# A bidirectional Mamba-2 layer with a low-rank FFN: five short steps change their place in the order of four engines

## The chip, the cores and the metric

The kernel runs on one core of one Trainium2 chip. The metric is the device time of one execution in microseconds (us). Five engines work side by side and meet through semaphores: PE (TensorE, matrix products; PEld are its weight loads), DVE (VectorE), ACT (ScalarE), POOL (GpSimd) and SP (SyncE, which here only issues DMAs). Each of them runs its own instructions strictly in the order in which they were written.

## The reference, cut to what matters

The input x is 8 sequences of 512 tokens with 256 features, all in float32. For each of two directions d (the second reads the sequence backwards):

```python
h0 = layernorm(x)
z, xBC, dt = split(h0 @ Win)               # 512, 640 and 8 columns
xs, B, C = split(silu(conv4(xBC) + convb)) # causal, 4 taps, per channel
dt = softplus(dt + dtb); dA = exp(-exp(Alog) * dt)
h_t = dA_t * h_(t-1) + dt_t * B_t x_t      # 8 heads of 64, state 64
y = C_t h_t + D * xs
y = y * silu(z)
y = y * rsqrt(mean(y * y) + 1e-5) * normw
out_d = y @ Wout
```

Then `x = x + concat(out_0, out_1) @ Wo + bo`, and last `x = x + FFN(layernorm(x))`, where `FFN(u) = u @ W.T + b + (u @ V_r) @ C.T`.

## The kernel before, in words

Each sequence is cut into four chunks of 128 tokens. A `Pair` is one chunk of the forward direction with the mirrored chunk of the backward one, so there are 8 x 4 = 32 pairs, and the main loop (L817 to L936) has one iteration for each, i = 4b + c. An iteration finishes pair i (`p`), prepares pair i+1 (`q`), does a part of the projections and convolutions of a later sequence (`work`, up to four `Block`s of 128 channels from the table `todo`), and carries the tails of finished chunks: a `Tail` is 128 tokens of output, from the product with the output weights to the FFN and the store. `t` holds the tails that begin in this iteration, `t0` those that began in the one before. `before` is pair i-1.

The steps that matter here, with their engines:

- `outputs` (L557, PE, L563): y of a pair. For c > 0 first the part that comes from the state, which reads the state `h` and the decays already multiplied by C (`dec`), then the part within the chunk, which reads `lam` and `xdt`. Results go to two banks of PSUM (`py`).
- `evict` (L591, DVE, L593) adds y to D * xs; `times_gate` (L595, POOL, L597) multiplies by silu(z); `square` (L599, ACT) squares; `presum` (L616, POOL, L618 and L619), `norm_sum` (L602, PE, L605), `norm_mean` (L607, ACT, L609) and `norm_power` (L611, POOL, L612) make 1/rms.
- `decay_state` (L549, POOL, L553) and `add_state` (L577): the state of the next chunk. `add_state` is a product on PE (L583) and then an addition on DVE (L588), or for c = 0 a copy on ACT (L586).
- `turn` (L492): transposes of x on PE (L496) and a copy on ACT for each direction (L498). `scale_x` (L500, POOL, L507) multiplies these copies by dt; `scan` (L483, DVE, L490) and `mix` (L519, DVE, L520) make `lam`; `scale_c` (L476, POOL, L479) makes `dec`.
- `skip` (L524, ACT, L528): D * xs, four instructions for each direction. `gate` and `gate_silu` (L532 and L544): z on PE and its silu on ACT.
- Of a block: `project` (PE, L379), `tap` (ACT, L390: the first of the four taps), `convolve` (DVE, L397, three instructions), `silu` (ACT, L415, or L423 for B and C).
- Of a tail: `bias1` (POOL, L633) adds bo to x; `project` (PE, L640) and `residual` (DVE, L647, then the statistics of L221 and L222); `scales` (POOL, L229 to L232) and `norm2` (ACT, L657) the second layer norm; `bias2` (POOL, L668) adds b to x; `turn` (PE, L673, and ACT, L675), `ffn` (PE, L680), `add_ffn` (DVE, L683) and `store` (SP, L686).
- `prepare_wf` (L207): once, in i=2, the FFN's low-rank product is made on PE (L212) and added to W on DVE (L213).

What sets the order is the text itself: `pin` (L60) makes each instruction of an engine follow the one traced before it. PSUM is handed out in pools of a few banks: three for projections, gates and the state's product (`p_proj`), two for transposes and small products (`p_tr`), two for `py`, `pm`, `pf` and the prepared weights (`p_y`). A new use of a bank waits until the engine that empties it is done. The second p_y bank of an iteration is that of `pm`, which `residual` empties.

Of the kernel before, what the change touches and what calls it, by code (L numbers as in the profile page):

```python
# [10 lines left out]
ALU = mybir.AluOpType  # L11
# [3 lines left out]
P = 128  # L15
NB, L, DM = 8, 512, 256
NC = L // P
DI = 512
# [13 lines left out]
def tile_bimamba_ffn(  # L32
# [39 lines left out]
    pe, dve, act, pool, sp = nc.tensor, nc.vector, nc.scalar, nc.gpsimd, nc.sync  # L72
# [4 lines left out]
    p_proj = ctx.enter_context(tc.tile_pool(name="p_proj", bufs=3, space=PSUM))  # L77
# [10 lines left out]
    def ps(p, shape, name):  # L88
        return p.tile(shape, F32, name=name, tag=p.name)
# [4 lines left out]
    def load(b, chunks=1):  # L94
        xt[b] = xin.tile([P, NC, DM], F32, name=f"x_{b}", tag="x")
        for c in range(0, NC, NC // chunks):
            cs = slice(c, c + NC // chunks)
            sp.dma_start(out=xt[b][:, cs], in_=x[b].rearrange("(c p) d -> p c d", p=P)[:, cs])
# [96 lines left out]
    def prepare_wy(d, blks):  # L195

        wot, wo_sb = staged[d]
        for blk in blks:
            pw = ps(p_y, [P, DM], f"pwy_{d}_{blk}")
            for k in range(NK):  # L200
                pe.matmul(
                    pw, lhsT=wot[:, k, blk * P:(blk + 1) * P], rhs=wo_sb[:, k, :],
                    start=(k == 0), stop=(k == NK - 1),
                )
            dve.tensor_scalar(wy[:, d, blk, :], pw, normw_sb[:, d, blk:blk + 1], None, ALU.mult)

    def prepare_wf():  # L207

        wt_sb, vt_sb, ct_sb = staged["ffn"]
        for k in range(NK):  # L210
            pw = ps(p_y, [P, DM], f"pwf_{k}")
            pe.matmul(pw, lhsT=vt_sb[:, k * P:(k + 1) * P], rhs=ct_sb, start=True, stop=True)  # L212
            dve.tensor_tensor(wf[:, k, :], pw, wt_sb[:, k, :], ALU.add)  # L213
# [23 lines left out]
    def stats1(b, c0):  # L237

        seq[b]["mv"] = statistics(xt[b], NC, f"ln1_{b}", range(c0, c0 + 2), seq[b].get("mv"))

    def scales1(b):
        seq[b]["rsnm"] = scales(seq[b].pop("mv"), NC, f"ln1_{b}")

    def norm1(b):
        rs, nm = seq[b].pop("rsnm")
        for c in range(NC):
            act.activation(
                xt[b][:, c, :], xt[b][:, c, :], AF.Identity, bias=nm[:, c:c + 1], scale=rs[:, c:c + 1]
            )

    def turn1(b, k):

        if k == 0:
            seq[b]["xhT"] = seqp.tile([P, NK, L], F32, name=f"xhT_{b}", tag="xhT", bufs=3)
        pt = ps(p_tr, [P, L], f"pxh_{b}_{k}")
        for c in range(NC):
            pe.transpose(pt[:, c * P:(c + 1) * P], xt[b][:, c, k * P:(k + 1) * P], ident)
        act.copy(seq[b]["xhT"][:, k, :], pt)
        if k == NK - 1:
            xt.pop(b)  # L260
# [81 lines left out]
    def steps_last(b0):  # L342
        g = seq[b0]["g"]
        last = g["last"] = sm("last", b0, (P, 64))
        act.activation(last[F], fold[F], AF.Copy, scale=upto[F, P:])
        act.activation(last[W], fold[W], AF.Copy, scale=onward[W, 0:1])
# [92 lines left out]
    class Pair:  # L439
# [137 lines left out]
        def add_state(m):  # L577
            if m.c == NC - 1:
                return
            pst = ps(p_proj, [P, DI], f"pst_{m.name}")  # L580
            for d in range(2):
                rows = slice(d * NS, (d + 1) * NS)
                pe.matmul(pst[rows, :], lhsT=m.s["bn"][:, m.c, rows], rhs=m.xw[d], start=True, stop=True)  # L583
            if m.c == 0:
                m.h_new = m.tile("h", (P, DI))
                act.copy(m.h_new, pst)  # L586
            else:
                dve.tensor_tensor(m.h_new, m.h_new, pst, ALU.add)  # L588
            m.s["h"] = m.h_new

        def evict(m, d):  # L591
# [163 lines left out]
    q = pairs[0]  # L755
# [51 lines left out]
    def when(t, *what):  # L807
        for one in t if isinstance(t, list) else [t]:
            if one is not None:
                for w in what:  # L810
                    getattr(one, w)()

    def begun(at):
        return [tails[j] for j in range(n) if begin[j] == at]

    st = late = before = None
    for i in range(n):  # L817
        p, q = pairs[i], pairs.get(i + 1)
        b, c = order[i]
        t, t0 = begun(i), begun(i - 1)  # L820
        work = todo.get((b, c), [])
        work = work + [None] * (4 - len(work))
        even = b % NSG == 0

        ahead = b + 2 if even else b + 1
        if i + 2 < n:
            if not (st and not even and c == 2):
                pairs[i + 2] = Pair(*order[i + 2])
                pairs[i + 2].fetch()
        if (c == 0 if even else c == 1) and b + 3 < NB:  # L830
            load(b + 3)
        when(t0, "scales", "norm2", "bias2")
        p.decay_state()
        p.outputs()
        for d in range(2):
            p.evict(d)
            p.times_gate(d)
        p.add_state()
        when(before, "norm_sum", "norm_mean")
        if q:  # L840
            for d in range(2):
                q.turn(d)
        when(work[0], "project", "tap")
        when(t0, "turn")
        for d in range(2):
            p.square(d)
        if even and c in (1, 3) and ahead < NB:
            norm1(ahead + (c == 3))
        when(late, "silu")
        if st and not even and c == 2:  # L850
            st.exponential()
        if q:
            q.cb()
            q.gate(0)
            q.gate_silu(0)
            for d in range(2):
                q.scale_x(d)
            q.scan(0)
        if q:
            q.scan(1)  # L860
            q.skip(0)
        when(work[0], "convolve", "silu")
        if i < 2:
            prepare_wy(i, range(2))
        if q:
            q.mix(0)
            q.mix(1)
        if st and not even and c == 2:
            st.decays()
            steps_last(ahead)  # L870
            pairs[i + 2] = Pair(*order[i + 2])
            pairs[i + 2].fetch()
        when(t0, "ffn", "add_ffn")
        when(before, "norm_power")
        if q:
            q.scale_c()
        when(t, "bias1")
        p.presum()
        if st and not even and c == 2:
            st.weigh()  # L880
        when(t, "project", "residual")
        if even and 1 <= c <= 2 and ahead + 1 < NB:
            stats1(ahead + 1, 2 * c - 2)
        if even and c == 0 and ahead < NB:
            stats1(ahead, 2)
            if b == 0:
                stats1(ahead, 0)
            scales1(ahead)
        if not even and c == 3 and b + 3 < NB:
            stats1(b + 3, 0)  # L890
        if even and c == 2 and ahead + 1 < NB:
            scales1(ahead + 1)
        when(work[1], "project", "tap")
        if i < 2:
            prepare_wy(i, range(2, NBLK))
        if q:
            q.skip(1)
        when(work[1], "convolve")
        if i == 2:
            prepare_wf()  # L900
        if i == 0:
            steps_last(0)
            steps_total(0)
        if not even and c == 3 and ahead < NB:
            steps_total(ahead)
        if st and not even and c == 1:
            st.ratio()
            st.series()
        if q:
            q.gate(1)  # L910
            q.gate_silu(1)
        if even and c in (1, 3) and ahead < NB:
            turn1(ahead + (c == 3), 0)
            turn1(ahead + (c == 3), 1)
        if c == 2 and b + 1 < NB:
            tokenwise_b(b + 1)
        when(work[1], "silu")
        for w in work[2:]:
            when(w, "project", "tap", "convolve")
        if b == 0:  # L920
            when(work[3], "silu")
        if st and not even and c == 2:
            steps_by_token(ahead)
            st = None
        late, before = work[2], p
        if i + 2 < n:
            pairs[i + 2].fetch_dec()
        when(t0, "store")
        for j in range(n):
            if begin[j] == i + 1:  # L930
                tails[j] = Tail(*ends[j])
                tails[j].load()
        if even and c == 3 and ahead < NB:
            st = Steps(ahead, *steps_v(ahead))
        pairs.pop(i)
        pin()  # L936


    t, t0 = begun(n), begun(n - 1)
# [52 lines left out]
```

## Time and profile before

| what | value |
|---|---|
| time, median of 3 runs | 665.66 us (665.1 to 667.6) |
| the profiled execution's own time | 668.52 us |
| its span, first to last instruction | 666.5 us |
| PE busy | 623.3 us, 94% of the span |
| DVE busy | 542.0 us, 81% |
| POOL busy | 467.2 us, 70% |
| ACT busy | 399.8 us, 60% |
| mean granted clock of TensorE | 0.983 |

The profile is of one execution, so durations from it are set against 668.52 us. A busy share is a mean over the whole span; matmuls are pipelined, so a busy PE is not PE at its peak. Where an engine is idle, the profile names what ended the wait, inferred from semaphores; of several semaphores it names the one that came last by its records.

### The profile page before, as it was taken

How to read it: one execution, taken by the hardware profiler on the slowest of the kernel's cores; microseconds unless marked ns; L12 is line 12 of the kernel's file. 1: busy time of each engine (PE TensorE's matmuls, PEld its weight loads, DVE VectorE, ACT ScalarE, POOL GpSimd, SP SyncE). 2: the span in 40 equal slices, each digit the busy share in tenths (PEclk: the TensorE clock that was granted, in tenths of full speed). 3: DMA queues.
4: the chain of work that ended last, by engine and by line, in shares of the span. 5: the costliest groups of instructions: out<-in, count | busy, mean ns of one | idle time of the engine just before them, and what ended most of it. 6: DMA issues, size and time to landing. Idle time of an engine off the chain costs nothing.

```text
span 666.5 us, 12446 instructions
## 1 busy us (share of the span) xinstructions
PE 623.3 (94%) x4652; PEld 478.5 (72%) x4652; DVE 542.0 (81%) x827; ACT 399.8 (60%) x855; POOL 467.2 (70%) x572
## 2 busy tenths in 40 slices
PE   4968998999999999999999999999999998999996
PEld 2556676777776777877777677777877777787785
DVE  4788888788988899977988998877998887886643
ACT  2787565876566565875476574686576654564421
POOL 4447455677854888757856789638876679599983
PEclk9979998999999999999999998999999998999998
DMA  7555332313055312134045322332005432333010
GB/s 207 161 168 143 111 104 49 86 42 102 18 182 142 112 62 90 59 92 143 17 135 147 92 64 80 112 112 103 25 13 179 104 111 80 111 112 111 17 49 32
DMA packets 34940, 64.63 MB, mean 97 GB/s; under 512 B 7680, under 2 KB 22080, under 8 KB 34880
## 3 DMA queue, kind: packets, MB, share of 16 engines
q1 hardware_dynamic: 32736, 63.79, 31.8%
q8 instruction: 37, 0.61, 0.4%
q10 hardware_dynamic: 2144, 0.04, 0.2%
q14 instruction: 23, 0.19, 0.1%
HBM read 59.10 MB, written 4.72 MB: 96 GB/s over the span
## 4 chain that ended last, share of the span: by engine, by line
PE 51%; DVE 24%; POOL 13%; ACT 7%; issue 4%; DVEq 0%; POOLq 0%; ACTq 0%
PE pm L640 11%; PE pp L379 9%; PE pz L538 9%; PE py L563 9%; DVE xc L397 7%; DVE lam L490 4%; PE pf L680 3%; POOL yg L597 3%; DVE lam L520 3%; PE pxs L496 3%; POOL xdt L507 2%; PE pdt L275 2%; DVE x L647 2%; ACT xc L390 2%; PE pst L583 2%
## 5 line engine op out<-in xcount | busy, mean ns | idle before, releaser
L397 DVE SCALAR_TENSOR_TENSOR xc<-pp,conv_sb,xc 128x511 f32<-128x511 f32 x183 | 136.0, 744 | 46.3 <-ACT xc L390 41.9
L379 PE MATMUL pp<-xhT,win_sb 128*128 128x512 f32 x320 | 151.2, 600 | 0.5 <-ACT xhT L710 0.5
L490 DVE TENSOR_TENSOR_SCAN lam<-lam,seed 128x512 f32<-128x512 f32 x128 | 145.6, 1200 | 0.0
L538 PEld LDWEIGHTS pz<-xhT,win_sb 128*128 128x128 f32 x1024 | 125.7, 194 | 10.3 <-issue 7.7
L538 PE MATMUL pz<-xhT,win_sb 128*128 128x128 f32 x1024 | 126.6, 277 | 0.0
L640 PE MATMUL pm<-wy,yg 128*128 128x256 f32 x512 | 115.5, 379 | 0.0
L640 PEld LDWEIGHTS pm<-wy,yg 128*128 128x128 f32 x512 | 97.1, 190 | 13.1
L379 PEld LDWEIGHTS pp<-xhT,win_sb 128*128 128x128 f32 x320 | 57.8, 194 | 45.7 <-issue 42.6
L528 ACT ACTIVATE yg<-xc,dcol 128x128 f32<-128x128 f32 x256 | 80.9, 393 | 0.0
L390 ACT ACTIVATE xc<-pp,conv_sb 128x512 f32<-128x512 f32 x64 | 49.3, 774 | 44.9 <-PE pp L379 44.7
L520 DVE TENSOR_TENSOR lam<-lam,cb 128x1024 f32<-128x1024 f32 x64 | 75.0, 1212 | 0.1
L668 POOL TENSOR_TENSOR x<-x,bf_sb 128x256 f32<-128x256 f32 x32 | 23.3, 729 | 73.6 <-ACT xh L657 71.5
L507 POOL TENSOR_TENSOR xdt<-xs,dw 128x512 f32<-128x512 f32 x64 | 66.5, 1046 | 6.6 <-ACT xs L498 6.6
L563 PE MATMUL py<-lam,xdt 128*64 128x128 f32 x1024 | 66.3, 285 | 0.0
L415 ACT ACTIVATE xc<-xc 128x512 f32<-128x512 f32 x64 | 39.5, 628 | 43.7 <-DVE xc L397 43.4
L563 PEld LDWEIGHTS py<-lam,xdt 128*64 128x64 f32 x1024 | 58.6, 143 | 7.5 <-issue 4.6
L593 DVE TENSOR_TENSOR yg<-py,yg 128x512 f32<-128x512 f32 x64 | 42.2, 685 | 18.0 <-PE py L563 15.5
L507 POOL TENSOR_TENSOR xs<-xs,dw 128x512 f32<-128x512 f32 x48 | 50.1, 1045 | 3.8
L647 DVE SCALAR_TENSOR_TENSOR x<-pm,rms,x 128x256 f32<-128x256 f32 x64 | 30.9, 483 | 25.4 <-POOL x L633 16.5
L496 PE MATMUL pxs<-ident,xc 128*128 128x128 f32 x256 | 39.7, 286 | 12.5 <-ACT rms L609 5.1
L498 ACT COPY xs<-pxs 128x512 f32<-128x512 f32 x64 | 36.1, 586 | 15.4 <-PE pxs L496 15.2
L496 PEld LDWEIGHTS pxs<-ident,xc 128*128 128x128 f32 x256 | 29.8, 151 | 19.2 <-ACT rms L609 6.8
(445 smaller groups left out, 996.0 us busy)
## 6 DMA issues: line engine op xcount, KB each, us to landing
lam<-dat SPq DMA_DIRECT2D x64, 512.0 KB, 5.2
x<-in_x_dram SPq DMA_DIRECT2D x36, 128.0 KB, 2.2
out_dram<-x SPq DMA_DIRECT2D x32, 128.0 KB, 1.7
x<-in_x_dram SPq DMA_DIRECT2D x7, 512.0 KB, 6.8
win_sb<-in_win_dram SPq DMA_DIRECT2D x2, 640.0 KB, 5.8
win_sb<-in_win_dram SPq DMA_DIRECT2D x2, 512.0 KB, 7.9
wot<-in_wout_t_dram SPq DMA_DIRECT2D x2, 512.0 KB, 12.4
wo_sb<-in_wo_dram SPq DMA_DIRECT2D x2, 256.0 KB, 8.9
```

The source lines that it names most:

```text
L379: pe.matmul(pp, lhsT=win_sb[:, d, k, c0:c0 + P], rhs=s["xhT"][:, k, :], start=(k == 0), stop=(k == NK - 1),)
L390: act.activation(self.acc, self.pp, AF.Identity, bias=self.w[:, 4:5], scale=self.w[:, 3:4])
L397: dve.scalar_tensor_tensor(self.acc[:, to], self.pp[:, of], self.w[:, 3 - j:4 - j], self.acc[:, to], ALU.mult, ALU.add,)
L490: dve.tensor_tensor_scan(lam, lam, sd, 0.0, ALU.mult, ALU.add)
L496: pe.transpose(pt[:, blk * P:(blk + 1) * P], m.s["xc", d][:, blk, m.tcol[d]], ident)
L507: pool.tensor_tensor(hb(to), hb(m.xw[d]), dw[:, j, cols].unsqueeze(2).to_broadcast([P, NH, HD]), ALU.mult)
L520: dve.tensor_tensor(m.lam[d], m.lam[d], m.pcb[:, d, :].unsqueeze(1).to_broadcast([P, NH, P]), ALU.mult)
L528: act.activation(yg[:, blk, :], m.s["xc", d][:, blk, m.tcol[d]], AF.Copy, scale=dcol[:, d, blk:blk + 1])
L538: pe.matmul(pz[:, blk, :], lhsT=win_sb[:, d, k, blk * P:(blk + 1) * P], rhs=m.s["xhT"][:, k, m.tcol[d]], start=(k == 0), stop=(k == NK - 1),)
L563: pe.matmul(m.py[d][two * HD:(two + 1) * HD, blk, :], lhsT=lhsT, rhs=rhs, start=first, stop=last, skip_group_check=True,)
L640: pe.matmul(t.pm[:, d, :], lhsT=yg[:, blk, :], rhs=wy[:, d, blk, :], start=(blk == 0), stop=(blk == NBLK - 1),)
L647: dve.scalar_tensor_tensor(t.x1[:, 0, :], t.pm[:, d, :], t.s["rs", d, t.c], t.x1[:, 0, :], ALU.mult, ALU.add)
```

## The change

Five edits, all in the order of steps; no instruction is added or dropped.

1. `add_state` keeps its product on PE; its addition (or copy) becomes a step of its own, `new_state`, written after `norm_sum` and `norm_mean` of the pair before.
2. For every iteration that has a block to project, `norm2` is written behind the two `turn`s of `q` instead of at the head of the iteration, and `bias2` behind the `scale_x` of both directions. The four `scales` stay at the head. From i=27 on, where there is no block left, both stay where they were.
3. `bias1` is written ahead of `norm_power` and `scale_c` instead of behind them.
4. `prepare_wf` is written right after the projection of the second block of i=2 instead of after that block's convolution.
5. `skip(1)` of `q` is written behind `gate_silu(1)` and the `turn1` of a coming sequence instead of ahead of the second block's convolution.

```diff
         def add_state(m):
             if m.c == NC - 1:
                 return
-            pst = ps(p_proj, [P, DI], f"pst_{m.name}")
+            pst = m.pst = ps(p_proj, [P, DI], f"pst_{m.name}")
...
+
+        def new_state(m):
+            if m.c == NC - 1:
+                return
             if m.c == 0:
                 m.h_new = m.tile("h", (P, DI))
-                act.copy(m.h_new, pst)
+                act.copy(m.h_new, m.pst)
             else:
-                dve.tensor_tensor(m.h_new, m.h_new, pst, ALU.add)
+                dve.tensor_tensor(m.h_new, m.h_new, m.pst, ALU.add)
             m.s["h"] = m.h_new
...
-        when(t0, "scales", "norm2", "bias2")
+        when(t0, "scales")
+        if work[0] is None:
+            when(t0, "norm2", "bias2")
         p.decay_state()
...
         p.add_state()
         when(before, "norm_sum", "norm_mean")
+        p.new_state()
         if q:
             for d in range(2):
                 q.turn(d)
+        if work[0] is not None:
+            when(t0, "norm2")
         when(work[0], "project", "tap")
...
             for d in range(2):
                 q.scale_x(d)
+        if work[0] is not None:
+            when(t0, "bias2")
+        if q:
             q.scan(0)
...
         when(t0, "ffn", "add_ffn")
+        when(t, "bias1")
         when(before, "norm_power")
         if q:
             q.scale_c()
-        when(t, "bias1")
         p.presum()
...
         if i < 2:
             prepare_wy(i, range(2, NBLK))
-        if q:
-            q.skip(1)
+        elif i == 2:
+            prepare_wf()
         when(work[1], "convolve")
-        if i == 2:
-            prepare_wf()
...
             turn1(ahead + (c == 3), 0)
             turn1(ahead + (c == 3), 1)
+        if q:
+            q.skip(1)
         if c == 2 and b + 1 < NB:
             tokenwise_b(b + 1)
```

## The prediction, made before the changed kernel was seen

> **What bounds the kernel now.** I number the iterations of the main loop i = 0 to 31 (i = 4b + c). First I read busy time by stretch of the span: start and length, then the busy time of PE, PEld, DVE, ACT and POOL.
>
> ```profile
> 263.00:326.00 63.00, 63.00 (x524) 49.58 (x524) 53.36 (x80) 42.86 (x92) 44.12 (x56) 1.00 0.33 99
> 326.00:402.00 76.00, 71.52 (x529) 54.29 (x527) 67.93 (x107) 49.56 (x107) 55.69 (x65) 1.00 0.33 99
> 573.00:641.00 68.00, 64.48 (x600) 53.84 (x599) 47.12 (x63) 34.17 (x82) 57.50 (x69) 1.00 0.29 86
> ```
>
> The loop repeats every eight iterations (154.3 us between the gate products of i=8 and i=16, 215.37 and 369.69). In its first half (263 to 326, i=11 to 13) PE is never idle. In the second (326 to 402, i=14 to 17) PE stands idle 4.5 us and DVE is the fullest. In the last six iterations POOL is. Then I read PE's idle gaps, in the timeline of PE (start, duration, instruction, idle time before it and what ended it):
>
> ```profile
> 110.95 1.97 PE L563 MATMUL py<-dec__866,h__873 64*64 64x128 f32 x32 [2.41 <-POOL ln_nm L232]
> ...
> 367.85 0.66 PE L496 MATMUL pxs<-ident,xc 128*128 128x128 f32 x4 [1.09 <-ACT rms L609]
> ...
> 399.73 0.63 PE L257 MATMUL pxh<-ident,x 128*128 128x128 f32 x4 [1.11 <-DVE lam L520]
> ...
> 401.10 1.43 PE L563 MATMUL py<-dec__3705,h__3724 64*64 64x128 f32 x28 [0.38 <-DVE x L647]
> ```
>
> The first is at the start of i=3. POOL's ln_nm only happens to end nearby; DVE shows the cause:
>
> ```profile
> 108.24 2.29 DVE L397 SCALAR_TENSOR_TENSOR xc<-pp,conv_sb,xc 128x511 f32<-128x511 f32 x3
> 110.44 0.75 DVE L213 TENSOR_TENSOR wf<-pwf,wt_sb 128x256 f32<-128x256 f32 x2
> ```
>
> The outputs of i=3 need the two banks of p_y that hold the FFN weights' product; DVE empties them only after a convolution. The last gap (401.10) is the same bank rule: the residual (L647) empties the second one. What makes that residual late is in the chain of waits:
>
> ```profile
> 376.40 0.72 POOL rms L612
> 377.12 2.34 POOL dec__3525 L479
> 379.46 0.70 POOL x L633
> 380.16 0.02 issue
> 380.18 0.49 DVE x L647
> ```
>
> DVE waits for bias1 (L633), which is queued on POOL behind norm_power (L612) and scale_c (L479). The list of waits totals it (us, times, longest), along with two that the change touches:
>
> ```profile
> POOL x L668 <- ACT xh L657: 71.5, 29, 8.8
> ...
> ACT rms L609 <- PE ss L605: 41.2, 19, 6.1
> ...
> DVE x L647 <- POOL x L633: 16.5, 10, 3.9
> ```
>
> The 71.5 us of POOL before bias2 looks largest, but POOL is not the bound before i=27, so I don't count it as time.
>
> **What the Trainium skill says.** "TensorE: Matmul & The Clock Gate", Part 1: the clock is either full or half, decided over free-running windows of 3.4 us by how busy PE was. The trace agrees: half clock for 3.41 us after 111.58, 401.71 and 555.31, each time after a window with PE busy 29, 56 and 47% (I cut the timeline at the steps of the clock); windows at 68% kept it. So a gap can cost its length and up to 1.7 us more. "Perfetto Trace Analysis", Optimization Strategy: with several regimes, look for the gaps within the regime that binds; that is what I do below.
>
> **The change, part by part.** No instruction is added or removed; 0 us of work.
>
> *prepare_wf before the convolution (i=2).* Both L213 run at about 108.3 instead of 110.44, the convolution 0.75 later. PE can start i=3's outputs at 109.05 (second bank empty) instead of 110.95 and, at full clock, ends them near 111.9 instead of 115.8. But the next convolution (111.95 to 114.27 before, now behind silu and tap of the one delayed) ends at about 114.95, and the last transpose of i=3 reads its output, so PE's next projection starts near 115.2 instead of 117.23: 2.0 us. PE then idles about 1.8 us in the clock window 111.58 to 114.99 (49% busy, below the 56% that halved it): the projection, 1.72 us, would take about 3.4, and 0.5 us is left. Both ends stand, 0.5 and 2.0; I take 1.0. i=3 to 5 are PE's, so it is kept.
>
> *bias1 ahead of norm_power and scale_c.* Together these take 3.06 us of POOL. bias2 moves in front of it with 0.7, so bias1 is done at about 377.8 in i=16 instead of 380.16, and L647 follows L683 directly. DVE wins the gap, 0.70 us, at once, as convolution, silu, tap, convolution and evict behind it follow each other. In i=17 another 0.15 (0.12 to 0.2 of the same gap): mix ends near 398.85, L647 near 400.2 instead of 401.05. So PE's outputs of i=18 go on 0.85 us earlier. Next in line is scale_c, now 1.4 us (two biases) later in POOL's queue: 399.33 - 0.7 + 1.4 = 400.05, just before L647's end. It fits by 0.15 us. i=8, 16 and 24 have this form: 3 x 0.85 = 2.55. In i=5, 13 and 21 L647 waits 0.11 to 0.13: 0.1 each, 0.3 (scale_c lands level with PE there, 322.4 against 322.33, so no more). The 2.2 us waits in i=4, 12, 20 lie where PE is full: nothing. In i=11's form norm_power, 1.4 later, is needed by L647, done near 279.75 for 280.66: 0.9 us of cover.
>
> *Sum of squares before the addition; norm2 behind the copies of x.* PE's order is the same. norm_mean no longer stands behind norm2 (0.6) and, for c = 0, h's copy (0.6): the gap at 367.85 shrinks by about 0.95, two others by up to 0.4. PE is not the bound there; it waits later for the same mix. Counted 0, as DVE's time covers it. norm2 is still done before its transposes: in c = 0 about 0.2 us earlier (copies end 293.8, norm2 294.4, transposes 294.67); were that cover gone it costs that much, at most 0.4 in 7 iterations.
>
> *bias2 later.* It no longer makes POOL wait in front of decay_state and times_gate; the state's addition on DVE waited 1.16 for that in i=10, where PE is full: 0. What waits now is scale_x no longer, only bias1 and scale_c behind it (above). add_ffn (L683) needs it: near 377.1 for 379.06.
>
> *skip(1) later.* Four ACT instructions (1.17 us together) move from before gate_silu(1) to after it and the copies of the turned x. Where gate_silu waits for PE, they now stand ahead of the convolution's silu, and so of the tap and next convolution. Margins between the end of skip and the need: i=14 1.2 us, i=15 1.1, i=16 3.0: nothing. In i=11 and i=3 about 0.5 late, i=12 level: PE's half, covered. In i=26 gate_silu can start only at 574.0, skip ends 575.7, the copy of B 576.1, silu 576.1 instead of 575.43: 0.55 lost, and i=27 starts POOL's stretch. It helps in i=0 (steps_total 1.2 us earlier), hidden behind DVE.
>
> *The end (i=27 to 31).* bias1 frees L647 by up to 3.0 us, so PE's stalls of 0.78 and 1.29 before L563 (i=29, 30) shrink, but POOL runs without a break from 592.9 to 612 and scale_c is 0.7 later: I find the last FFN matmuls 0.7 earlier, less the 0.55 of i=26, about 0.2. Bounds -0.6 and +1.0.
>
> The DMAs stay where they were on SP's queue; none is moved past another, and fetches depend on buffers that come free no later. SP: 0.
>
> Sum: 1.0 + 2.55 + 0.3 + 0.2 = 4.05 us. The profiled execution took 668.52 us, 2.0 more than its span of 666.48; less 4.05 is 664.5. It stands 2.86 above the median of the runs shown, 665.66; so 661.6.
>
> **Rivals.** *Fuller gain*: the clock stays full at 115 (2.0) and isn't halved at one of the two later places (1.3, as 3.25 us against 1.97 for the outputs of i=18), and the end gives 1.0: 2.0 + 2.85 + 1.3 + 1.0 = 7.15, 658.5. For it: halving hangs on where the window falls (i=9 has i=17's gaps and kept its clock). *The wait moves to scale_c*: 0.15 us of cover is thin; if multiplied decays land 0.6 later, i=8, 16, 24 give 0.25 each, with 0.5, 0.3 and -0.6 the rest: 0.95, 664.7. *Slower*: skip(1) delays a convolution where DVE binds. It decides once gate_silu's start plus 0.5 and 1.17 (and 0.44 for B's copy) passes the end of the convolution before; 1.17 us twice in each of 3.5 periods is 8.2, less 4.05: 4.1 slower, 669.8. Against it: margins of 1.1 to 3.0 us in i=14 to 16.
>
> **Chances.** Likeliest 0.52 (660.0 to 663.4), fuller 0.22, wait moved 0.20, slower 0.06. The range, 658.2 to 665.1, leaves out slower and the outer part of fuller and moved. Half a per cent, about what a measurement can tell from no change, is 3.3 us, so faster begins at 662.3: two thirds of the likeliest plus fuller, 0.56; same, the other third and moved, 0.38; slower 0.06.
>
> **What would show it.** L213 at about 108.3, and the gap before L563 at 111 down to about 0.5, with a new one of 1.8 before the last pxs; no wait of L647 for L633 in i=16 to 30 (except i=27, where norm_power is needed); i=8 to 16 apart by 153.3 to 153.5 us. Wrong if L563 of i=17/18 waits for L479, if POOL's ACT wait returns elsewhere, or if DVE's idle before L397 grows past 1.43 in i=14 to 17.

## The result, and the profile after

The changed kernel takes **659.19 us** in the median of 5 runs (658.52 to 660.46), against 665.1 (662.96 to 667.6) for the kernel before in the same comparison: a ratio of 0.9914 [0.9888, 0.994]. A later comparison, of 6 runs against 11, gave 658.76 against 665.59, 0.9900 [0.9876, 0.9925]. So the change saves 5.9 to 6.8 us. The forecast was 661.6 in a range of 658.2 to 665.1; the likeliest case reached from 660.0 to 663.4, and the result lies next to the rival "fuller gain" (658.5).

The profiled execution took 660.46 us (span 658.4, mean clock 0.990); that of the kernel before took 668.52 (666.5, 0.983). The line numbers move by four from `evict` on: `evict` is now L597, `times_gate` L601, the sum of squares L609, `norm_mean` L613, `norm_power` L616, `bias1` L637, the residual L651, `bias2` L672, `add_ffn` L687. First the idle gaps of PE in the changed kernel (start, duration, instruction, idle time before it and what ended it), at the same places as in the prediction and at two later ones:

```profile
116.13 0.33 PE L496 MATMUL pxs<-ident,xc 128*128 128x128 f32 x1 [1.55 <-DVE xc L397]
...
365.10 0.66 PE L496 MATMUL pxs<-ident,xc 128*128 128x128 f32 x4 [0.18 <-ACT rms L613]
...
397.16 0.63 PE L257 MATMUL pxh<-ident,x 128*128 128x128 f32 x4 [1.66 <-DVE lam L520]
398.22 1.20 PE L563 MATMUL py<-dec__3705,h__3721 64*64 64x128 f32 x32 [0.44 <-POOL dec__3705 L479]
...
613.35 1.20 PE L563 MATMUL py<-dec__5864,h__5883 64*64 64x128 f32 x32 [1.62 <-POOL dec__5864 L479]
```

The 2.41 us before the outputs of i=3 are gone, and 1.55 stand a little later, before the last transposes of x. The gap that `norm_mean` left (1.09 at 367.85) is down to 0.18. Before the outputs of i=18, where PE waited 0.38 for the residual, it now waits 0.44 for `scale_c` (L479), and the gap ahead of that has grown from 1.11 to 1.66.

DVE just before PE starts i=3: both sums of the FFN weights now run ahead of the convolution.

```profile
109.38 0.72 DVE L213 TENSOR_TENSOR wf<-pwf,wt_sb 128x256 f32<-128x256 f32 x2
110.02 2.31 DVE L397 SCALAR_TENSOR_TENSOR xc<-pp,conv_sb,xc 128x511 f32<-128x511 f32 x3
```

POOL in i=16, where the kernel before ran `norm_power`, `scale_c` and only then `bias1`:

```profile
374.70 0.73 POOL L672 TENSOR_TENSOR x<-x,bf_sb 128x256 f32<-128x256 f32 x1
375.38 0.73 POOL L637 TENSOR_TENSOR x<-x,bo_sb 128x256 f32<-128x256 f32 x1
376.08 0.72 POOL L616 TENSOR_TENSOR rms<-rms,neghalf 128x2 f32<-128x2 f32 x1
376.77 2.37 POOL L479 TENSOR_TENSOR dec__3525<-dec__3525,cc 128x1024 f32<-128x1024 f32 x1
```

and what DVE does meanwhile:

```profile
377.28 0.42 DVE L687 TENSOR_TENSOR x<-pf,x 128x256 f32<-128x256 f32 x1
377.62 1.00 DVE L651 SCALAR_TENSOR_TENSOR x<-pm,rms,x 128x256 f32<-128x256 f32 x2
```

`bias1` ends at 376.1, over a microsecond before the residual needs it, and L651 follows L687 without a gap. The list of waits (total us, times, longest) has no line for the residual behind `bias1` any more, which was 16.5 us in 10 waits. The 71.5 us that POOL waited before `bias2` haven't vanished. Most have gone to the gate product, from 44.7 us to 114.6:

```profile
POOL yg L601 <- DVE yg L597: 114.6, 26, 8.9
...
ACT rms L613 <- PE ss L609: 48.8, 22, 5.4
...
POOL x L672 <- ACT xh L661: 7.3, 6, 3.8
```

That is idle time of an engine that isn't the bound there: it changes its name, and the runs below find no gain from it. PE's stretches, moved along with the iterations (start and length, then busy time of PE, PEld, DVE, ACT and POOL, clock, DMA share, GB/s):

```profile
261.10:324.10 63.00, 63.00 (x526) 49.53 (x524) 52.99 (x79) 42.19 (x91) 44.02 (x57) 1.00 0.33 99
324.10:400.00 75.90, 71.70 (x541) 54.89 (x541) 68.56 (x109) 50.14 (x108) 55.23 (x65) 1.00 0.34 102
566.00:634.00 68.00, 64.21 (x601) 53.89 (x600) 47.02 (x63) 33.55 (x83) 57.35 (x69) 1.00 0.29 89
```

They are much like before: i=11 to 13 belong to PE, and in i=14 to 17 PE still stands idle 4.2 us. What was saved is small at each place, and it is found by laying the starts of the iterations of both traces side by side:

| PE starts the outputs of | before | after | lead | what was won or lost since the line above |
|---|---|---|---|---|
| i=1 | 71.91 | 69.61 | 2.31 | 1.1 lie before i=0; 1.2 from `skip(1)`, given back in i=1 |
| i=2 | 92.41 | 93.89 | -1.48 | half clock from 75.95 to 82.78 |
| i=4 | 134.38 | 133.44 | 0.93 | FFN weights, at full clock |
| i=8 | 208.58 | 207.64 | 0.94 | nothing |
| i=12 | 288.74 | 286.87 | 1.88 | `bias1` in i=8 and 9 |
| i=16 | 362.90 | 361.06 | 1.84 | nothing |
| i=20 | 444.68 | 440.29 | 4.39 | `bias1` 0.9; 1.65 as the clock isn't halved |
| i=28 | 589.67 | 582.72 | 6.95 | `bias1` 0.9; 1.65 as the clock isn't halved |
| end of the span | 666.48 | 658.45 | 8.03 | 0.45 in i=29 to 31; 0.6 clock |

Nearly all the mechanisms of the prediction are there, each close to its size. What this pair of executions adds is the clock.

### The profile page after: what moved, and what is told of

The parts are those of the page before. It is cut to its first block, busy times and chain, and to the rows that moved or that the text cites. A ratio compares the mean times of both kernels' runs of the same rounds, so it can differ in the third digit from the quotient of the medians.

```text
span 658.4 us, 12499 instructions
## 1 busy us (share of the span) xinstructions
PE 617.1 (94%) x4652; PEld 474.4 (72%) x4652; DVE 541.6 (82%) x827; ACT 399.0 (61%) x855; POOL 465.7 (71%) x572
## 3 DMA queue, kind: packets, MB, share of 16 engines
q1 hardware_dynamic: 32736, 63.79, 31.9%
## 4 chain that ended last, share of the span: by engine, by line
PE 48%; DVE 26%; POOL 12%; ACT 7%; issue 4%; DMA 1%; SPq 0%; POOLq 0%; ACTq 0%; DVEq 0%
PE pp L379 11%; PE pm L644 9%; PE pz L538 8%; DVE xc L397 8%; PE py L563 6%; DVE lam L490 6%; DVE lam L520 3%; PE pxs L496 3%; PE pf L684 3%; PE pdt L275 2%; POOL xdt L507 2%; POOL yg L601 2%; ACT xc L390 2%; DVE yg L597 2%; PE pst L583 2%
## 5 line engine op out<-in xcount | busy, mean ns | idle before, releaser
L397 DVE SCALAR_TENSOR_TENSOR xc<-pp,conv_sb,xc 128x511 f32<-128x511 f32 x183 | 136.2, 745 | 52.6 <-ACT xc L390 48.2
L563 PE MATMUL py<-lam,xdt 128*64 128x128 f32 x1024 | 63.0, 276 | 0.0
L563 PEld LDWEIGHTS py<-lam,xdt 128*64 128x64 f32 x1024 | 55.2, 137 | 7.1 <-issue 4.3
L597 DVE TENSOR_TENSOR yg<-py,yg 128x512 f32<-128x512 f32 x64 | 41.8, 684 | 14.8 <-PE py L563 13.0
L651 DVE SCALAR_TENSOR_TENSOR x<-pm,rms,x 128x256 f32<-128x256 f32 x64 | 30.8, 481 | 13.7 <-PE pm L644 8.0
L613 ACT ACTIVATE rms<-ss,eps_col 128x2 f32<-128x2 f32 x32 | 8.3, 260 | 49.2 <-PE ss L609 48.8
## 6 DMA issues: line engine op xcount, KB each, us to landing
wot<-in_wout_t_dram SPq DMA_DIRECT2D x2, 512.0 KB, 12.6
```

Source lines behind the costliest of these rows:

```text
L397: dve.scalar_tensor_tensor(self.acc[:, to], self.pp[:, of], self.w[:, 3 - j:4 - j], self.acc[:, to], ALU.mult, ALU.add,)
L563: pe.matmul(m.py[d][two * HD:(two + 1) * HD, blk, :], lhsT=lhsT, rhs=rhs, start=first, stop=last, skip_group_check=True,)
L597: dve.tensor_tensor(yg, m.py[d], yg, ALU.add)
```

## How much of it is the clock

The clock's part can be had from every run, as each lists its mean granted clock and its span. The clock is either full or half, so the time at half clock is 2 x (1 - mean clock) x span. For the profiled run of before that is 2 x 0.017 x 666.5 = 22.7 us, and its trace shows 22.4 (one stretch of 6.8, three of 3.4, and the last 5.4). The clock is given to 0.001, so one value is good to 0.7 us; the means below are better.

Within the runs of one kernel the spans follow this time: in 57 runs of the kernel before it is mostly near 18.6 us (spans around 663.4) or near 22.6 (around 665.5). Pooled over all kernels a microsecond at half clock goes with 0.41 us of span. "TensorE: Matmul & The Clock Gate", Terms, puts the penalty of throttled time at that time x (1 - the granted share), here 0.5; the runs stay a little below, as they would where PE isn't the bound. Kernel by kernel the slope scatters (0.48 for the kernel before, 0.06 for the six runs of only_bias1), so a single row is rough. With 0.41 to 0.5, the difference of the mean spans splits like this (edits numbered as in the change):

| kernel | runs | half clock, us | mean span, us | against before | of it clock | the rest |
|---|---|---|---|---|---|---|
| before | 57 | 19.5 | 664.0 | | | |
| after (all five edits) | 11 | 11.7 | 657.3 | -6.7 | -3.2 to -3.9 | -3.5 to -2.8 |
| only_bias1 (3) | 6 | 12.9 | 657.1 | -6.9 | -2.7 to -3.3 | -4.2 to -3.6 |
| only_wf (4) | 12 | 14.0 | 661.0 | -3.0 | -2.3 to -2.8 | -0.7 to -0.2 |
| only_norm (1, 2) | 6 | 24.2 | 673.0 | +9.0 | +1.9 to +2.4 | +7.1 to +6.6 |
| only_skip (5) | 22 | 19.8 | 664.2 | +0.2 | +0.1 | +0.1 |
| no_bias1 (1, 2, 4, 5) | 5 | 31.1 | 675.2 | +11.2 | +4.8 to +5.8 | +6.4 to +5.4 |
| no_norm (3, 4, 5) | 6 | 11.4 | 657.3 | -6.7 | -3.3 to -4.1 | -3.4 to -2.6 |
| no_skip (1 to 4) | 5 | 12.6 | 656.1 | -7.9 | -2.8 to -3.5 | -5.1 to -4.4 |
| bw (3, 4) | 6 | 10.3 | 655.5 | -8.5 | -3.8 to -4.6 | -4.7 to -3.9 |

About half of what the change saves is time at full clock in place of half clock. The split is a regression over executions, not an experiment that holds the clock. The table of leads supports it by another way: what the change wins there without the clock is 0.45 for the FFN weights (the size they have at half clock, measured below), 3 x 0.93 for `bias1` and 0.45 at the end, together 3.7 us.

## The experiments

Ratios are of medians against the kernel before on the same chip, with their 95% intervals. **My theory** was that edit 3 brings most, edit 4 about 1 us, edits 1, 2 and 5 nothing. **The rivals** were that `scale_c` takes over the wait, that `skip(1)` costs a convolution, and that the clock makes the difference.

### Edit 3 alone (only_bias1)

```diff
+        when(t, "bias1")
         when(before, "norm_power")
         if q:
             q.scale_c()
-        when(t, "bias1")
         p.presum()
```

> The kernel before with bias1 alone moved ahead of norm_power and scale_c. Theory A (bias1 frees the residual, which the second bank of p_y waits for): about 3.5 us faster, 0.85 us in each of i=8, 16 and 24 and up to 1 us in the last five iterations; L647 no longer waits for L633 except in i=27. Rival B (what counts is POOL freed from its wait for norm2): within 1 us of before. Rival C (the gain is the PE clock not being halved): no fixed gain, only as many us as half-clock windows are missing, about 1.6 each.

Measured: 659.04 us (657.99 to 660.08), ratio **0.9899 [0.9878, 0.9919]**. This one line, alone, brings as much as the five edits. PE in its trace, before the outputs of i=10 and of i=18:

```profile
242.07 0.63 PE L257 MATMUL pxh<-ident,x 128*128 128x128 f32 x4 [0.70 <-DVE lam L520]
243.22 1.09 PE L563 MATMUL py<-dec__2165,h__2184 64*64 64x128 f32 x28 [0.16 <-DVE x L647]
...
395.13 0.63 PE L257 MATMUL pxh<-ident,x 128*128 128x128 f32 x4 [0.70 <-DVE lam L520]
396.28 1.09 PE L563 MATMUL py<-dec__3705,h__3724 64*64 64x128 f32 x28 [0.16 <-DVE x L647]
```

Both gaps are smaller than before (1.11 and 0.38), whereas in the changed kernel they are larger (1.66 and 0.44), so it is the other edits that widen them. The lead over the kernel before grows by 0.75 at i=10, 18 and 26, which I had predicted, and by 0.5, 0.5 and 0.3 at i=7, 15 and 23, which I hadn't. The clock isn't halved between 115 and 650 us. Of the 7.2 us, the 3.6 to 4.2 apart from the clock are what theory A expected (3.5); rival C has the other 2.7 to 3.3.

### Edit 4 alone (only_wf)

```diff
         if i < 2:
             prepare_wy(i, range(2, NBLK))
+        elif i == 2:
+            prepare_wf()
         if q:
             q.skip(1)
         when(work[1], "convolve")
-        if i == 2:
-            prepare_wf()
```

> The kernel before with prepare_wf alone moved ahead of the second block's convolution. Theory A: 2.0 us faster where the clock stays full after PE's new gap near 115 us, 0.5 us where it is halved; nothing after i=5 differs. Rival: DVE is the bound through i=2 and i=3, so the 0.75 us by which the convolution starts later is handed on and nothing is gained.

Measured: 663.36 us (659.28 to 664.7), **0.9951 [0.9934, 0.9968]**. PE in its trace:

```profile
107.94 1.38 PE L563 MATMUL py<-dec__866,h__873 64*64 64x128 f32 x32 [0.17 <-POOL ln_rs L229]
...
114.19 0.47 PE L496 MATMUL pxs<-ident,xc 128*128 128x128 f32 x1 [1.55 <-DVE xc L397]
```

The clock is halved from 114.18 on, and the lead over the kernel before grows by 0.45 us (0.77 to 1.21) between i=2 and i=4: the lower bound of the prediction, and its mechanism. The other 3.3 us of this pair of traces are two halvings at i=18 and i=26 that the kernel before had and this execution hadn't, with PE's gaps in front of them unchanged (1.11 and 0.37). The table above says the same of all 12 runs: 5.5 us less half clock, hardly any rest.

### Edits 1 and 2 alone (only_norm), and everything but edit 3 (no_bias1)

`norm2` and `bias2` stand where the whole change puts them.

```diff
             if m.c == 0:
                 m.h_new = m.tile("h", (P, DI))
-                act.copy(m.h_new, pst)
+                act.copy(m.h_new, m.pst)
...
-        when(t0, "scales", "norm2", "bias2")
+        when(t0, "scales")
+        if work[0] is None:
+            when(t0, "norm2", "bias2")
...
         when(before, "norm_sum", "norm_mean")
+        p.new_state()
```

> The kernel before with the sum of squares in front of the state's addition and with norm2 and bias2 moved, nothing else. Theory A: within 0.5 us of before, although POOL's wait for norm2 (71.5 us) nearly disappears; PE's gap before the second transposes of i=16 shrinks by 0.9 us and comes back before the turned x of i=17. Rival B: 3 us or more faster. A loss of 0.5 to 1.5 us is possible too, since bias2 now stands in front of bias1 and scale_c on POOL.

Measured: 674.71 us (671.89 to 677.06), **1.0127 [1.0101, 1.0154]**, 8.5 us slower. DVE's residual in i=8, and PE before the outputs of i=10:

```profile
227.36 1.00 DVE L651 SCALAR_TENSOR_TENSOR x<-pm,rms,x 128x256 f32<-128x256 f32 x2 [1.48 <-POOL x L637]
...
249.00 1.97 PE L563 MATMUL py<-dec__2165,h__2181 64*64 64x128 f32 x28 [1.10 <-DVE x L651]
```

The wait for `bias1` there was 0.71 before and is 1.48; PE's gap was 0.38 and is 1.10. POOL's queue in i=8 is now `bias2`, `norm_power`, `scale_c`, `bias1`, so that the instruction DVE waits for comes one bias (0.73) later. In the whole run the residual waits for `bias1` 21.6 us in 16 waits, against 16.5 in 10. Against the kernel before PE is 0.75 late at i=8 and 1.5 at i=10. By i=11 a third 0.75 has come; no_bias1's trace shows it alone, and in only_norm a halving of 6.8 us at 248.5 adds 3.0 to it. Each of the two later periods of eight iterations costs another 2.2 or 2.3. Without the halving that is 6.7 us, the rest of 6.6 to 7.1 in the table. So theory A is wrong, and the loss that it called possible is far larger than its 0.5 to 1.5. No run moves `bias2` alone: that it makes the loss, and not edit 1 or `norm2`, is read from this wait.

In the other direction, the changed kernel with `bias1` put back behind `scale_c`:

```diff
-        when(t, "bias1")
         when(before, "norm_power")
         if q:
             q.scale_c()
+        when(t, "bias1")
```

> The changed kernel with bias1 put back behind norm_power and scale_c. Theory A (what pays is that the residual no longer waits for bias1, and moving bias2 costs 0.72 us of POOL in front of bias1 in each iteration where DVE waits for it): slower than the kernel before by 4 to 7 us (only_norm's 8.5 less only_wf's 2.9). Rival B (each edit pays for itself): between the changed kernel and the kernel before.

Measured: 677.41 us (674.1 to 678.91), **1.018 [1.015, 1.021]**. Four of the five edits together are 11.3 us slower than the kernel before, and edit 3 is worth 18 us on top of them, but 7 on its own. About half of the 11.3 and of the 18 is half clock (31.1 us against 19.5 and 11.7). Edits 2 and 3 aren't two terms of a sum: edit 2 lengthens the queue that edit 3 takes `bias1` out of.

### Edit 5 alone (only_skip)

```diff
             prepare_wy(i, range(2, NBLK))
-        if q:
-            q.skip(1)
         when(work[1], "convolve")
...
             turn1(ahead + (c == 3), 1)
+        if q:
+            q.skip(1)
```

> The kernel before with skip(1) alone moved behind gate_silu(1). Theory A: 0.5 us slower, by the evict of i=27 (0.55 us later relative to i=25), and PE arrives 1.2 us earlier in i=1 and waits there as much longer, which can halve its clock and cost up to 2.3 us more. Rival: it is faster, because the copies of the turned x come earlier.

Measured: 666.23 us (663.33 to 669.43, 22 runs), **1.0002 [0.9989, 1.0015]**. In the trace `evict` after i=26 is 0.5 later, where the prediction had 0.55; i=14 to 16 move not at all. In i=1 PE gets ahead by 1.2 and then waits 2.49 for `norm_mean` in place of 1.32. The clock of this execution is then halved from 77.21 on, but the mean of the 22 runs has no more half clock than before (19.8 us, 19.5).

### Leaving out one edit of the five (no_norm, no_skip), and edits 3 and 4 only (bw)

> The changed kernel with norm2 and bias2 back at the head of the iteration and the sum of squares back behind the addition; bias1, prepare_wf and skip(1) stay moved. Theory A (bias2 in front of bias1 and scale_c only costs): faster than the changed kernel by 1 to 3 us, as the multiplied decays come 0.7 us earlier and PE's gaps before L563 in i=10, 18 and 26 shrink. Rival B (with bias1 first, taking norm2 out of PE's way pays): slower than the changed kernel by 1 us or more.

> The changed kernel with skip(1) back ahead of the convolution. Theory A: faster than the changed kernel by 0.5 us at i=27 and by up to 2.3 us where PE's clock was halved in i=1; PE's gap at the second transposes of i=1 goes back from 2.5 to 1.3 us. Rival: no difference that can be told.

> The kernel before with bias1 and prepare_wf alone moved. Theory A (these two carry the gain, the others cost): about 656 us on this chip, the sum of the two alone (7.2 and 2.9 less what both owe to the clock), 2 to 4 us below the changed kernel. Rival B (the norm and the skip help once bias1 is first): above the changed kernel.

Measured: without edits 1 and 2, 659.69 us (657.44 to 660.35), 0.9902 [0.9878, 0.9926]; without edit 5, 658.42 (656.98 to 658.76), 0.9884 [0.9859, 0.9908]; with edits 3 and 4 alone **657.59** (655.35 to 659.25), **0.9875 [0.9849, 0.9901]**. With `bias1` in front, edits 1 and 2 make no difference to the time (0.9902 beside 0.9900), so both theories about no_norm, 1 to 3 us faster and 1 us or more slower, missed. Edit 5 seems to cost something: in the column of the rest 1.3 to 1.6 us, with and without edits 1 and 2. In the traces I find 1.0 of it. The lead over the kernel before, won by PE in four stretches of the loop, in us:

| kernel | i=6 to 8 | i=14 to 16 | i=22 to 24 | i=28 to 31 |
|---|---|---|---|---|
| bw (3, 4) | 0.55 | 0.52 | 0.30 | 0.89 |
| no_norm (3, 4, 5) | 0.34 | 0.34 | 0.11 | 0.44 |
| no_skip (1 to 4) | 0.24 | 0.12 | 0.22 | 0.93 |
| after (all) | 0.04 | 0.01 | 0.02 | 0.45 |

Edit 5 takes 0.1 to 0.2 us in each of the first three and 0.45 in the last; edits 1 and 2 take 0.1 to 0.4 in the first three. The whole change gives back all that edit 3 wins in these three. In two stretches between them, i=8 to 12 and 16 to 20, edits 1 and 2 win 0.16 each. So bw is ahead by 2.26 less 0.52 less 0.32, 1.4 us, which goes with the medians, 657.59 against 659.19 and 658.76; but the intervals overlap, so "1 to 2 us faster than the change" is likely and not shown. The 2 to 4 us that bw was expected to win are too many.

### Does the gap before i=10 and i=18 halve the clock? (after_again, warm)

The gaps of 1.66 and 0.44 in the changed kernel looked like a trap. The first run here is the changed kernel once more. The second repeats four of the transposes in front of the gap four times, which leaves the result as it is:

```diff
-            pe.transpose(pt[:, c * P:(c + 1) * P], xt[b][:, c, k * P:(k + 1) * P], ident)
+            for _ in range(4 if k == 0 and b in (4, 6) else 1):
+                pe.transpose(pt[:, c * P:(c + 1) * P], xt[b][:, c, k * P:(k + 1) * P], ident)
```

> The changed kernel once more, beside the next three on one chip. Theory A: 0.9 to 1.0% faster than before; the profile differs from the first only by where the clock is halved: PE's gaps of 1.7 and 0.4 us in i=9 and 17 fall into one clock window in about 3 of 4 placements of the window, and i=10 or i=18 is then 1.6 us longer. Rival: no halving there again, so the change itself prevents it.

> The changed kernel with the first half of the turned x of i=9 and i=17 transposed four times instead of once (same result, 1.3 us of PE more each, in the gap where PE waits for the mix). Theory A (the clock is lost to gaps): the gap of 1.66 us becomes about 0.35, no half clock in i=10 or i=18 and 1 to 2.5 us faster in the median than the changed kernel. Rival (a gap costs its length only): same time or slower.

Measured: after_again 658.76 us, 0.9900 [0.9876, 0.9925]; warm 660.19 (657.22 to 661.38), 0.9905 [0.9878, 0.9932]. The edit did what it was for:

```profile
393.23 0.63 PE L258 MATMUL pxh<-ident,x 128*128 128x128 f32 x4 [0.35 <-DVE lam L521]
394.31 1.20 PE L564 MATMUL py<-dec__3717,h__3733 64*64 64x128 f32 x32 [0.45 <-POOL dec__3717 L480]
```

The expected gain isn't there: a miss. The time at half clock is no lower (12.7 us against 11.7). So most of the changed kernel's half clock isn't made at these gaps. The filler is transposes; whether these count for the clock as other products do is not tested. Its two traces show 6.8 us near 41 us, where the first chunks are prepared, and the rest in i=1, once at i=10 and at the end.

Whether a gap halves the clock hangs on where the free-running windows of 3.41 us fall. The windows of after_again around the start of i=10, then around that of i=18 (columns as above; the clock is the third from the right):

```profile
239.16:242.58 3.42, 1.33 (x27) 1.10 (x30) 3.31 (x8) 2.04 (x6) 3.42 (x3) 1.00 0.12 40
242.58:245.99 3.41, 3.41 (x42) 3.08 (x36) 1.51 (x6) 0.69 (x3) 3.00 (x7) 0.50 0.89 319
392.76:396.18 3.42, 1.76 (x17) 1.55 (x16) 3.42 (x5) 1.89 (x5) 3.42 (x4) 1.00 0.00 0
396.18:399.59 3.41, 2.99 (x63) 2.58 (x63) 2.68 (x9) 1.76 (x5) 3.16 (x5) 1.00 0.66 205
```

The same work with the same gaps leaves PE busy 39% of a window at i=10, and the next runs at half clock; at i=18 two windows share the gaps, the emptier has 51%, and the clock stays full. In the changed kernel's first trace they were shared in both places:

```profile
239.79:243.20 3.41, 2.28 (x21) 2.04 (x19) 3.37 (x4) 2.71 (x7) 3.41 (x5) 1.00 0.00 0
243.20:246.62 3.42, 2.45 (x48) 2.07 (x50) 3.20 (x10) 1.76 (x5) 3.34 (x3) 1.00 0.45 128
393.39:396.81 3.42, 2.11 (x19) 1.87 (x18) 3.38 (x4) 2.53 (x7) 3.42 (x5) 1.00 0.00 0
396.81:400.22 3.41, 2.62 (x52) 2.25 (x54) 3.01 (x10) 1.76 (x5) 3.32 (x3) 1.00 0.43 153
```

So the change doesn't prevent a halving there; this execution escaped it. "TensorE: Matmul & The Clock Gate", Part 1, calls the window free-running, which is what these runs show: within a trace all steps of the clock before the end lie whole windows apart, but the first halving starts at 41.82 us in one trace of the changed kernel and at 41.19 in the other.

### Is scale_c the new bound? (sc_first, bw_sc)

`norm_power` is put behind `scale_c`, which is then 0.7 earlier, in the changed kernel (sc_first) and in the one with edits 3 and 4 only (bw_sc):

```diff
         when(t, "bias1")
-        when(before, "norm_power")
         if q:
             q.scale_c()
+        when(before, "norm_power")
```

> The changed kernel with norm_power behind scale_c. Theory A (what is late next is scale_c, as PE's gaps before L563 in i=10, 18, 26, 29 and 30 name it): those gaps are 0.4 to 0.7 us shorter, 1.5 to 2.5 us faster than the changed kernel. Rival: the residual or the mix is due right behind, and less than 0.5 us is gained.

> bias1 and prepare_wf moved, and norm_power behind scale_c, nothing else. Theory A: the fastest of all, 0.5 to 1.5 us below bias1 and prepare_wf alone, from i=26, 29 and 30, where PE waited 0.4, 0.2 and 1.65 us for scale_c. Rival: POOL binds from i=27 on and its sum is unchanged, so nothing is gained.

Measured: sc_first 659.43 us (658.1 to 660.62), 0.9903 [0.9882, 0.9925], no gain. bw_sc **656.75** (656.51 to 659.76), **0.9873 [0.985, 0.9897]**: the lowest median of all, though not to be told from bw. PE in sc_first, before the outputs of i=18:

```profile
396.81 1.09 PE L563 MATMUL py<-dec__3705,h__3721 64*64 64x128 f32 x28 [0.16 <-DVE x L651]
```

The wait for `scale_c` is gone, and the residual ends the next one, level with it. From i=10 to 28 DVE's evicts keep their distance to those of the changed kernel within 0.1 us. In i=29 and 30 they come 0.7 earlier, and in i=31 that is lost again; the gap for `scale_c` there shrinks only from 1.62 to 1.45. In bw_sc PE wins 1.4 us from i=28 to 31, against 0.9 in bw, but at the end of the span both have won the same 1.26. So the rivals, that the next wait is due right behind and that nothing is gained at the end, fit better than the theories.

## Why the prediction was nearly right, point by point

- **bias1 first** (3 x 0.85). Right, with its mechanism: 0.93 in each of i=8-9, 16-17 and 24-25 in the changed kernel, 0.8 with the edit alone. `bias1` was to be done near 377.8; less the lead of 1.9 by then that is 375.9, and it ends at 376.1. The 0.1 in i=5, 13 and 21 didn't come: the edit alone wins 0.3 to 0.5 an iteration or two later, and the other edits take that back.
- **scale_c next in line.** I had it ready 0.15 before the residual's end. It comes about level: it ends at 398.2, and the residual at 398.26. The sign I named as one that would prove me wrong, L563 of i=17 and 18 waiting for L479, is there, with 0.44 us. Its price is nearly nothing, as sc_first shows, so the rival "the wait moves" has its place right and its price wrong.
- **prepare_wf.** Both bounds were met: 0.45 where the clock was halved (only_wf), 2.1 to 2.4 where it wasn't (the changed kernel). The gap before L563 fell to under 0.2 us rather than 0.5, and the new one is 1.55 rather than 1.8. L213 ran at 109.38 for 108.3, as this execution was 1.5 us late by i=2. I priced the halving by "49% busy, below the 56% that halved it"; the window from 113.50 had 55% and kept its clock, and in the kernel before one with 52% (from 63.79) had kept it too. So 1.0 between the two bounds was a guess.
- **Edits 1 and 2** (0). Right for the change: the gap behind `norm_mean` shrank by 0.9 as worked out, for nothing in time. It holds only because `bias1` moved as well. I had `bias2`'s 0.7 in front of `bias1` in the sum and didn't see that it decides the sign: without edit 3 the two edits cost 8.5 us. POOL's wait did return elsewhere, which I had named as a sign of being wrong, and it cost nothing.
- **skip(1)** (0.55 in i=26, 0 elsewhere). The 0.5 is there. DVE's idle before L397 in i=14 to 17 didn't grow (1.42, 2.72 and 1.42 us; before 1.42, 2.72 and 1.43, so the limit of 1.43 that I set was passed from the start). But the margins in i=14 to 16 were not as wide as I had them: once `bias1` is early, the edit takes 0.1 to 0.2 us in each of i=6 to 8, 14 to 16 and 22 to 24.
- **The end** (+0.2): 0.45 from i=28 on. Inside the bounds.
- **The clock: the term that was mis-sized.** I let it cut the gain at 115 and otherwise counted it at nothing; 1.3 for one place stood in a rival. In the runs the time at half clock falls by 7.8 us, worth 3.2 to 3.9. The rest, 2.8 to 3.5 (3.7 by the leads), is somewhat less than the 4.05 of the sum. The forecast of 661.6 for 659.2 is thus a sum near enough with a clock term left out. The likeliest case, 660.0 to 663.4, missed the median by 0.8 for that reason, and the median's nearness to "fuller gain" doesn't prove that rival's arithmetic.

**What stays open.** Why the half clock falls so much. From the traces I had counted how often a window with little work (PE busy below 57.5%, between 60 and 650 us) would occur if windows fell anywhere with equal chance: 3.6 times in the changed kernel, 2.6 before. The runs show the opposite, less half clock after. Either the places of the windows are not independent of the program, or busy time alone doesn't decide.

For edit 3 the traces give a part of the answer. Between 125 and 600 us the same count (below 58%) is 1.2 before and 0 in only_bias1, bw, no_norm and bw_sc: wherever a window is laid there, PE is busy at least 66% of it, and none of these four traces has a halving there. The kernel before has two. Edits 1 and 2 widen the gaps again: the count is 1.5 in the changed kernel (no halving in one trace, one in the other) and 3.1 in only_norm and no_bias1 (three and one). So edit 3 takes this half clock away and edits 1 and 2 bring the chance of it back; that the changed kernel has so little all the same, and no more than warm, whose count is 0 again, is not explained. Nor is it shown why edit 4, which works in i=2 and leaves this count at 1.2, goes with 5.5 us less half clock over the whole run.

## What to carry to other kernels

In an in-order queue, put the step that another engine waits for ahead of those needed later, and then price every step that the same edit moves ahead of it: edits 1 and 2, which put 0.73 us of `bias2` into POOL's queue ahead of `bias1`, cost 8.5 us while `bias1` stood last there and nothing that can be told once it stood before `norm_power` and `scale_c`. So edits to one queue are tested together and apart. Where PE has short gaps, take the mean clock of every run beside its span: 2 x (1 - clock) x span tells how much of a difference is half clock, which one pair of traces can't. And a wait that appears with a new name behind the one removed isn't a loss until something after it starts later.

## What the runs showed of the hardware that was not expected

- No sharp share of a window decides the clock. Halvings followed windows in which PE was busy 29, 39, 47, 56, 57 and 58%; windows with 51% (shown above), 52% (warm, from 606.2) and 55 and 56% (the changed kernel, from 113.5 and 611.9) kept full clock. In all 14 traces together, from 50 us on: of the windows at full clock, 25 of the 26 in which PE was busy less than 49% were followed by half clock, 9 of the 35 with 49 to 59%, and none of the 2402 with more.
- Most halvings last one window, 3.41 us, and cost 1.6 us where PE is the bound; some last two: 6.8 us at 248.5 in only_norm, from 75.95 in the changed kernel. Coming back took more work than staying: from 50 us on, the nine windows at half clock in which PE was busy 41 to 85% were followed by more half clock, and the 21 with 96% or more by full clock. (One earlier window, from 46.49 in only_skip, came back with 82%.)
- The time at half clock of one and the same kernel falls into groups: in 48 of the 57 runs of the kernel before it is near 18.6 or 22.6 us, with spans about 2 us apart. This is most of the spread of its runs.
